# Layer 1's softmax divided on GpSimd before its product with the values, in a two-layer attention and feed-forward kernel

## The chip, the cores and the metric

The kernel runs on one core of a Trainium2 chip, in one launch. The metric is the device time of that launch in microseconds, the median of several runs. The engines are named as the profile names them: PE (TensorE, matmuls and transposes), PEld (its weight loads), DVE (VectorE), ACT (ScalarE), POOL (GpSimd) and SP (SyncE, which issues DMAs).

## The reference, cut to what matters

Input x has 2 batches of 2048 rows of 512 numbers, that is 32 tiles of 128 rows. Two layers follow each other. Each has attention over a context of 128 rows and then a feed-forward part; a layer norm stands ahead of each of the four. Layer 0 has attention with rotary embedding and a quantised feed-forward part. Layer 1 is where the change lies:

```python
Q, K, V = heads(q @ Wq.T + bq), heads(k @ Wk.T + bk), heads(v @ Wv.T + bv)   # 16 heads of 32
scores = einsum('bhqd,bhkd->bhqk', Q, K) / sqrt(32)
scores = where(mask, 1e-9, scores)
attn = softmax(scores, axis=-1)
ctx = einsum('bhqk,bhkd->bhqd', attn, V)
x = x + (ctx @ Wo.T + bo)
# then, on the norm of x:
probs = softmax(x @ Wg + bg)                  # 512 wide
idx = argmax(probs); p = probs[idx]; e = idx % 8
out = relu(x @ We[e] + be[e]) * p             # the expert of each row
x = x + out
```

All arithmetic around the change is in float32. A softmax is exponentials divided by their sum over the 128 keys; the division may be made before the product with V or after it.

## The kernel before, in words

The first part of the launch (layer 0, up to about 944 us) is not touched. From there to 1476 us the kernel runs 32 steps, n = 0 to 31, one for each tile of 128 rows. The rest is the experts' work.

The order of instructions on PE, DVE, ACT and POOL is that of the code in this part: the schedule is manual (L741), each engine takes its instructions in the order in which the step issues them, and waits on semaphores where it needs another engine's result. A step does the attention of tile n, the output projection and the norm of tile n-1, the gate of tile n-2, and the layer norm of a tile that comes four later. Its functions, in the order of the loop (L1160 on):

- `weighed(n-1)`: DVE multiplies the attention's output `po` of the last step by reciprocals (L897).
- `scores(n)`: 16 small matmuls into `sc` (L833); DVE masks them into the tiles `s1_0` and `s1_1`, 8 heads of 128 keys each (L841), and takes their maxima (L846).
- `queries`: PE's product for the next block of two tiles (L813); it comes twice in a step.
- `exponentials(n)`: ACT makes 16 exponentials of 128x128 (L855). Those of the first half add up their rows as they go, by an accumulator that is read after each; those of the second half do not.
- `projected(n-1)`: POOL adds the bias `bob` to the residual (L902), PE multiplies by the output weights (L905), DVE adds the product to the residual (L906).
- `normed2(n-1)`: DVE takes mean and variance, POOL raises the variance to the power -0.5 (L100), DVE centres the tile (L103).
- `kept_keys(n+1)`: DVE turns a mask's row into numbers (L823). `normed`: the same statistics, power and centring for a tile of the block after the next.
- `logits(n-2)`: PE's gate product (L928); DVE's maximum and index (L930 to L934).
- `summed(n)`: DVE sums the second half's rows (L859) and takes the reciprocal of all 16 sums (L861); POOL spreads them to 128x512 (L864).
- `gated(n-2)`: ACT's exponentials of the gate with their sum (L942); DVE's expert number, its one-hot row `hot` (L949) and the running count `cum` (L950).
- for n from 4 to 19, POOL adds a row to two 128x512 pieces of the experts' weights (L1204).
- `turned(n)`: PE transposes the exponentials, 16 of 128x128, in four groups (L115); ACT copies each group back into `s1_0` and `s1_1` (L874).
- `turned2(n-1)`: PE transposes the centred tile (L115), ACT copies it (L922).
- `mixed(n)`: PE transposes the spread reciprocals into `pr` (L883), multiplies the exponentials by the values into `po` (L887), and ACT copies `pr` to `oT` (L892).
- in odd steps up to 27, `turned1` transposes the two tiles of the block after the next.

In steps 24 to 27 pieces of the routing table follow at the step's end, on DVE for the most part; in steps 30 and 31 an expert's product takes the queries' place. PE's results go to PSUM, in a ring of four buffers of 128x512 that all these products share, besides `sc` with one buffer. POOL cannot take part in work on PSUM here: all its operands are tiles in SBUF.

Of the kernel before, what the change touches and what calls it, by code (L numbers as in the profile page):

```python
# [11 lines left out]
F32 = mybir.dt.float32  # L12
# [6 lines left out]
ALU = mybir.AluOpType  # L19
# [4 lines left out]
P = 128  # L24
# [38 lines left out]
def two_layers(ctx: ExitStack, tc: tile.TileContext, a, out):  # L63
# [86 lines left out]
    with ExitStack() as l0:  # L150
# [168 lines left out]
        def normed(k):  # L319


            for t, n in enumerate(tiles[k]):
                mv = variance(xs[n])
                ve = small.tile([P, 1], F32, name="ve")
                nc.vector.tensor_scalar(ve, mv[:, 1:2], 1.0 + EPS, EPS * EPS, ALU.mult, ALU.add)
                rr = small.tile([P, 1], F32, name="rr")
                nc.gpsimd.tensor_tensor(rr, ve, minus_half, ALU.pow)
                norms[k, t] = mv, rr
# [84 lines left out]
        def projected(u, t):  # L413

            k, g = divmod(u, NG)
            if g == 0:
                pws[k, t] = psq.tile([P, D], F32, name="pw", tag="pw", bufs=NB0)
            pw = pws[k, t]
            for f in range(2):
                nc.tensor.matmul(  # L420
                    pw, atts[u][:, f, t * P : (t + 1) * P], wo[:, 2 * g + f, :],
                    start=(g == 0 and f == 0), stop=(g == NG - 1 and f == 1),
                )
# [356 lines left out]
        nc.gpsimd.tensor_tensor(xs[n], xs[n], y, ALU.add)  # L780


    scs, xTs, qTs, keeps, ss_, sums, rw_, pTs_, mix, os_ = {}, {}, {}, {}, {}, {}, {}, {}, {}, {}
    xn1s = {}

    def normed(n):
# [62 lines left out]
    def exponentials(n):  # L849

        sums[n] = small.tile([P, 16], F32, name="sums")
        for half, (s, mx) in enumerate(ss_[n]):
            for h in range(8):
                accum = {} if half else {"accum_out": sums[n][:, h : h + 1]}
                nc.scalar.activation(s[:, h, :], s[:, h, :], AF.Exp, bias=mx[:, h : h + 1], **accum)  # L855

    def summed(n):

        nc.vector.tensor_reduce(sums[n][:, 8:], ss_[n][1][0], AX.X, ALU.add)  # L859
        rs = small.tile([P, 4, 4], F32, name="rs")  # L860
        nc.vector.reciprocal(rs, sums[n].rearrange("p (r c) -> p c r", c=4))  # L861

        rw_[n] = mid.tile([P, 4, P], F32, name="rw", bufs=1)
        nc.gpsimd.tensor_copy(  # L864
            rw_[n].rearrange("p c (r f) -> p c r f", f=DH1), rs.unsqueeze(3).to_broadcast([P, 4, 4, DH1])
        )

    def turned(n):

# [7 lines left out]
    def mixed(n):  # L877

        b, pTs = n // TPB, pTs_[n]
        pr = psm.tile([P, 4, P], F32, name="pr1", tag="m")  # L880
        po = psm.tile([P, 4, P], F32, name="po1", tag="m")
        for c in range(4):
            nc.tensor.transpose(pr[:, c, :], rw_[n][:, c, :], ident)  # L883
        for c in range(4):
            for r in range(4):
                h = 4 * c + r
                nc.tensor.matmul(  # L887
                    po[32 * r : 32 * r + 32, c, :], v1[b][:, h * DH1 : (h + 1) * DH1], pTs[r][:, c, :],
                    start=True, stop=True, tile_position=(0, 32 * r),
                )  # L890
        oT = mid.tile([P, 4, P], F32, name="oT", bufs=1)
        nc.scalar.copy(oT, pr)  # L892
        mix[n] = po, oT

    def weighed(n):
        po, oT = mix[n]
        nc.vector.tensor_tensor(oT, po, oT, ALU.mult)  # L897
        os_[n] = oT

    def projected(n):  # L900

        nc.gpsimd.tensor_tensor(xs[n], xs[n], bob, ALU.add)  # L902
        pw = psm.tile([P, D], F32, name="pw1", tag="m")
        for c in range(ND):
            nc.tensor.matmul(pw, os_[n][:, c, :], wo1[:, c, :], start=(c == 0), stop=(c == ND - 1))  # L905
        nc.vector.tensor_tensor(xs[n], xs[n], pw, ALU.add)  # L906
# [3 lines left out]
    def normed2(n):  # L910

        mv = variance(xs[n])
        nc.vector.tensor_copy(xw[n][:, D : D + 1], mv[:, 0:1])
        r = xw[n][:, D + 1 : D + 2]
        rsqrt_eps(r, mv[:, 1:2])
        xn2[n] = mid.tile([P, D], F32, name="xn2", bufs=1)
        return lambda: center(xn2[n], xs[n], mv[:, 0:1], r)
# [6 lines left out]
    def logits(n):  # L924

        pl = pls[n] = psm.tile([P, D], F32, name="pl", tag="m")
        for c in range(ND):
            nc.tensor.matmul(pl, xn2T[n][:, c, :], wgate[:, c, :], start=(c == 0), stop=(c == ND - 1))  # L928
        m8 = small.tile([P, 8], F32, name="m8")
        nc.vector.max(out=m8, in_=pl)  # L930
        negm = small.tile([P, 1], F32, name="negm")
        nc.vector.tensor_scalar(negm, m8[:, 0:1], -1.0, None, ALU.mult)
        i8 = small.tile([P, 8], U32, name="i8")
        nc.vector.max_index(out=i8, in_max=m8, in_values=pl)  # L934
        picks[n] = negm, i8

    def gated(n):

        negm, i8 = picks[n]
        pe = small.tile([P, 1], F32, name="pe1")  # L940

        nc.scalar.activation(  # L942
            scs[min(n + 2, NT - 1)][:, 0].rearrange("p c k -> p (c k)"), pls[n], AF.Exp, bias=negm, accum_out=pe
        )
        ei = small.tile([P, 1], U32, name="ei")
        nc.vector.tensor_scalar(ei, i8[:, 0:1], NE - 1, None, ALU.bitwise_and)
        ef = small.tile([P, 1], F32, name="ef")
        nc.vector.tensor_copy(ef, ei)
        nc.vector.tensor_scalar(hot[:, n, :], iota_e, ef, None, ALU.is_equal)  # L949
        nc.vector.tensor_tensor(cum[:, n + 1, :], cum[:, n, :], hot[:, n, :], ALU.add)  # L950
        nc.vector.memset(xw[n][:, D + 3 : D + 4], 0.0)

        def rest():
            nc.vector.reciprocal(xw[n][:, D + 2 : D + 3], pe)
            nc.sync.dma_start(out=x_dram[n * P : (n + 1) * P, :], in_=xw[n])

        return rest
# [202 lines left out]
    for n in range(NT):  # L1160
        blk, t = n // NB1, n % NB1
        ahead = blk + 1 < nblk
        fs = range(t * ND // NB1, (t + 1) * ND // NB1)
        if n > 0:
            weighed(n - 1)
        scores(n)
        if ahead:
            queries(blk + 1, fs[:1])
        exponentials(n)
        if n == 0:  # L1170
            for i in range(NT - held, NT - held + 2):
                down(i)
                widened(i + 2)
        if n > 0:
            projected(n - 1)
            rest2 = normed2(n - 1)
        if n + 1 < NT:
            kept_keys(n + 1)
        rest1 = normed((blk + 2) * NB1 + t) if blk + 2 < nblk else None
        if n > 0:  # L1180
            rest2()
        if n > 1:
            logits(n - 2)
        summed(n)
        rest = gated(n - 2) if n > 1 else None
        if rest1:
            rest1()
        if ahead:
            queries(blk + 1, fs[1:])
        if n == 0:  # L1190
            for i in range(NT - held + 2, NT):
                down(i)
            dwn.close()
            ffd.close()
            moe = ctx.enter_context(tc.tile_pool(name="moe", bufs=1, side="right"))
            we = moe.tile([P, NE, ND, D], F32, name="we")
            for e in range(NE):
                load(we[:, e], a["L1_ffn_We"][e].rearrange("(c p) f -> p c f", p=P))
        if 4 <= n < 4 + 2 * NE:
            e, half = divmod(n - 4, 2)  # L1200
            if half == 0:
                load(rowadd, v_dram[e].partition_broadcast(P))
            for c in range(2 * half, 2 * half + 2):
                nc.gpsimd.tensor_tensor(we[:, e, c, :], we[:, e, c, :], rowadd, ALU.add)  # L1204
        if not ahead:

            expert(n - NT + NB1)
        turned(n)
        if rest:
            rest()  # L1210
        if n > 0:
            turned2(n - 1)
        mixed(n)
        if t == NB1 - 1 and blk + 2 < nblk:
            for t in range(NB1):
                turned1((blk + 2) * NB1 + t)
        if n == NTA + 2:
            route = routing(True)
        if route:
            for _ in range(3 if n == NTA + 2 else 2):  # L1220
                if next(route, route) is route:
                    route = None
                    for j in range(4):
                        gathered(j)
                    break
        if n == NT - NB1 - 1:
            for j in range(2):
                centered_x(j)
            turned_x2(0)
    weighed(NT - 1)  # L1230
    projected(NT - 1)
    normed2(NT - 1)()
    logits(NT - 2)
# [50 lines left out]
```

## Time and profile before

| what | time |
| --- | --- |
| median of 3 runs | 1643.19 us (1642.39 to 1645.04) |
| the profiled execution | 1642.48 us |
| its span, first to last instruction | 1640.8 us |
| 32 attention steps of layer 1 | 944 to 1476 us |
| step 20, scores to scores | 15.74 us |
| step 21 (odd: two more tiles turned) | 16.77 us |
| mean granted clock of TensorE | 0.998 |

The profile is one execution. A row gives an engine's instruction with its source line, what it writes and reads, and its duration. Matmuls are pipelined, so a PE row's duration overlaps the next one; the distance between starts tells what a piece of work takes of PE. "Waits" say which engine's semaphore ended an idle time.

### The profile page before, as it was taken

How to read it: one execution, taken by the hardware profiler on the slowest of the kernel's cores; microseconds unless marked ns; L12 is line 12 of the kernel's file. 1: busy time of each engine (PE TensorE's matmuls, PEld its weight loads, DVE VectorE, ACT ScalarE, POOL GpSimd, SP SyncE). 2: the span in 40 equal slices, each digit the busy share in tenths (PEclk: the TensorE clock that was granted, in tenths of full speed). 3: DMA queues.
4: the chain of work that ended last, by engine and by line, in shares of the span. 5: the costliest groups of instructions: out<-in, count | busy, mean ns of one | idle time of the engine just before them, and what ended most of it. 6: DMA issues, size and time to landing. Idle time of an engine off the chain costs nothing. (4 is left out here: it accounts for less than half of the span.)

```text
span 1640.8 us, 26515 instructions
## 1 busy us (share of the span) xinstructions
PE 1597.7 (97%) x9962; PEld 952.5 (58%) x9962; DVE 1185.9 (72%) x2290; ACT 686.3 (42%) x1539; POOL 437.5 (27%) x498
## 2 busy tenths in 40 slices
PE   7999999999999999989999999999999999999997
PEld 5666666665666666534443566666666666654543
DVE  3466666777777765689986678898999889876332
ACT  1222222222222222234436576666666665662332
POOL 2322222222222221110005632333333221224553
PEclk9999999999999999999999999999999999999999
DMA  9400111010100220556658650001000000113332
GB/s 318 151 17 22 28 26 27 20 27 20 27 20 14 54 37 1 161 161 183 186 175 294 235 204 16 27 20 33 21 27 20 21 14 21 40 47 103 125 124 67
DMA packets 123883, 128.61 MB, mean 78 GB/s; under 512 B 43857, under 2 KB 91433, under 8 KB 123756
## 3 DMA queue, kind: packets, MB, share of 16 engines
q1 hardware_dynamic: 114508, 107.03, 21.2%
q0 software_dynamic: 6240, 18.70, 3.6%
q8 instruction: 80, 1.31, 0.3%
q10 hardware_dynamic: 3008, 1.19, 0.3%
q14 instruction: 47, 0.39, 0.1%
HBM read 78.96 MB, written 41.76 MB: 74 GB/s over the span
## 5 line engine op out<-in xcount | busy, mean ns | idle before, releaser
L362 PE MATMUL pq<-xnT,wq 128*128 128x256 f32 x1024 | 254.4, 392 | 0.0
L420 PE MATMUL pw<-wo,att 128*128 128x512 f32 x512 | 230.9, 593 | 0.0
L362 PEld LDWEIGHTS pq<-xnT,wq 128*128 128x128 f32 x1024 | 184.6, 190 | 66.9 <-issue 46.7
L855 ACT ACTIVATE s<-s,mx 128x128 f32<-128x128 f32 x512 | 176.7, 387 | 18.1 <-DVE mx L846 18.1
L388 ACT ACTIVATE pr<-sc 128x1024 f32<-128x1024 f32 x64 | 65.5, 1024 | 237.8 <-PE sc L383 234.7
L372 POOL TENSOR_TENSOR q<-rt,rt 128x256 f32<-128x256 f32 x64 | 46.5, 726 | 410.5 <-DVE rt L371 410.5
L420 PEld LDWEIGHTS pw<-wo,att 128*128 128x128 f32 x512 | 97.0, 190 | 96.2 <-issue 89.8
L410 DVE RECIPROCAL rd<-sc 128x256 f32<-128x256 f32 x64 | 112.5, 1757 | 51.1 <-PE sc L404 51.1
L1119 PE MATMUL pz<-we,x 128*128 x312 | 140.7, 594 | 0.6 <-issue 0.5
L813 PE MATMUL pq<-xT,wq 128*128 128x256 f32 x512 | 124.1, 385 | 0.0
L347 ACT ACTIVATE xnT<-pt,lnb,lng 128x256 f32<-128x256 f32 x64 | 32.6, 559 | 216.1 <-PE pt L345 216.1
L367 DVE TENSOR_TENSOR rt<-pq,rope_cos 128x256 f32<-128x256 f32 x64 | 27.2, 425 | 130.8 <-PE pq L362 120.2
L905 PE MATMUL pw<-wo,oT 128*128 128x512 f32 x256 | 115.5, 594 | 1.6 <-DVE oT L897 1.6
L928 PE MATMUL pl<-wgate,xnT 128*128 128x512 f32 x256 | 115.1, 592 | 0.0
L813 PEld LDWEIGHTS pq<-xT,wq 128*128 128x128 f32 x512 | 94.9, 190 | 28.0 <-issue 13.6
L716 ACT ACTIVATE gate<-pg,gsc 128x512 f32<-128x512 f32 x88 | 60.5, 687 | 96.5 <-PE pg L711 85.8
L711 PE MATMUL pu<-xqT,wuT 128*128 128x512 bf16 x352 | 90.3, 379 | 5.3 <-DVE h L719 5.3
L91 DVE BATCH_NORM_STATS2 st<-x 128x6 f32<-128x512 f32 x130 | 89.6, 689 | 5.6 <-DMA x<-in_ctx 3.4
L841 DVE SCALAR_TENSOR_TENSOR s<-sc,keep 128x1024 f32<-128x1024 f32 x64 | 77.9, 1217 | 20.6 <-PE sc L833 20.6
L1123 DVE TENSOR_TENSOR x<-x,x 128x512 f32<-128x512 f32 x39 | 27.0, 692 | 90.0 <-ACT x L1122 89.8
L711 PE MATMUL pg<-xqT,wgT 128*128 128x512 bf16 x352 | 90.3, 379 | 0.0
L1119 PEld LDWEIGHTS pz<-we,x 128*128 128x128 f32 x312 | 56.4, 190 | 58.2 <-issue 57.9
(218 smaller groups left out, 2847.7 us busy)
## 6 DMA issues: line engine op xcount, KB each, us to landing
h_dram<-h SPq DMA_DIRECT2D x88, 256.0 KB
hq<-h_dram SPq DMA_DIRECT2D x31, 704.0 KB
x_dram<-x SPq DMA_DIRECT2D x32, 258.0 KB
x<-in_x SPq DMA_DIRECT2D x32, 256.0 KB
we<-in_L_ffn_We SPq DMA_DIRECT2D x8, 1024.0 KB
w_in<-in_L_ffn_w_gate SPq DMA_DIRECT2D x11, 256.0 KB
w_down<-in_L_ffn_w_down SPq DMA_DIRECT2D x4, 704.0 KB
w_in<-in_L_ffn_w_up SPq DMA_DIRECT2D x11, 256.0 KB
```

The lines of the kernel that those rows point to most:

```text
L91: nc.vector.bn_stats(out=st, in_=x)
L362: nc.tensor.matmul(pq, wqs[c // 2][:, c % 2, par, g * P : (g + 1) * P], xnTs[k][:, c, :], start=(c == 0), stop=(c == ND - 1))
L388: nc.scalar.activation(pr, sc[:, :, :B0], AF.Tanh, scale=1.0 / (math.sqrt(DH0) * GROK))
L410: nc.vector.reciprocal(rd, sc[:, 0, B0:])
L420: nc.tensor.matmul(pw, atts[u][:, f, t * P : (t + 1) * P], wo[:, 2 * g + f, :], start=(g == 0 and f == 0), stop=(g == NG - 1 and f == 1),)
L711: nc.tensor.matmul(dst, w[:, c, i * P : (i + 1) * P], xqTs[blk][:, c, :], start=(c == 0), stop=(c == ND - 1),)
L813: nc.tensor.matmul(pq, wq1[:, c, f * P : (f + 1) * P], xTs[blk][:, c, :], start=(c == 0), stop=(c == ND - 1))
L841: nc.vector.scalar_tensor_tensor(s, sc[:, 2 * half : 2 * half + 2].rearrange("p r c k -> p (r c) k"), -MASKED, keeps[n].unsqueeze(1).to_br ...
L855: nc.scalar.activation(s[:, h, :], s[:, h, :], AF.Exp, bias=mx[:, h : h + 1], **accum)
L905: nc.tensor.matmul(pw, os_[n][:, c, :], wo1[:, c, :], start=(c == 0), stop=(c == ND - 1))
L928: nc.tensor.matmul(pl, xn2T[n][:, c, :], wgate[:, c, :], start=(c == 0), stop=(c == ND - 1))
L1119: nc.tensor.matmul(pz, ring[j][:, c, :], we[:, bass.ds(e, 1), c, :], start=(c == 0), stop=(c == ND - 1))
```

## The change

The exponentials themselves are divided by their sums before they are transposed, on POOL, one product for each half of the heads; the reciprocals are no longer spread, turned and copied. ACT's accumulators now go with the second half, and DVE sums the first. The output projection's PSUM result is copied by ACT alone, and `weighed` is gone. In a step the gate's product now comes ahead of the output's, the bias is added in a function of its own ahead of the two products on POOL, and the centring of tile n-1 follows its statistics at once. `kept_keys` and the other norm's statistics come after the gate. The counts of experts (`cum`) are added by POOL.

```diff
-    def summed(n):
-        nc.vector.tensor_reduce(sums[n][:, 8:], ss_[n][1][0], AX.X, ALU.add)
-        rs = small.tile([P, 4, 4], F32, name="rs")
-        nc.vector.reciprocal(rs, sums[n].rearrange("p (r c) -> p c r", c=4))
-        rw_[n] = mid.tile([P, 4, P], F32, name="rw", bufs=1)
-        nc.gpsimd.tensor_copy(
-            rw_[n].rearrange("p c (r f) -> p c r f", f=DH1), rs.unsqueeze(3).to_broadcast([P, 4, 4, DH1])
-        )
+    def shares(n, half):
+        s, sm = ss_[n][half][0], sums[n][:, 8 * half : 8 * half + 8]
+        if half == 0:
+            nc.vector.tensor_reduce(sm, s, AX.X, ALU.add)
+        rs = small.tile([P, 8], F32, name="rs")
+        nc.vector.reciprocal(rs, sm)
+        nc.gpsimd.tensor_tensor(s, s, rs.unsqueeze(2).to_broadcast([P, 8, T]), ALU.mult)
...
     def mixed(n):
-        pr = psm.tile([P, 4, P], F32, name="pr1", tag="m")
         po = psm.tile([P, 4, P], F32, name="po1", tag="m")
-        for c in range(4):
-            nc.tensor.transpose(pr[:, c, :], rw_[n][:, c, :], ident)
...
-        oT = mid.tile([P, 4, P], F32, name="oT", bufs=1)
-        nc.scalar.copy(oT, pr)
-        mix[n] = po, oT
-
-    def weighed(n):
-        po, oT = mix[n]
-        nc.vector.tensor_tensor(oT, po, oT, ALU.mult)
-        os_[n] = oT
+        os_[n] = mid.tile([P, 4, P], F32, name="oT", bufs=1)
+        nc.scalar.copy(os_[n], po)
+
+    def biased(n):
+        nc.gpsimd.tensor_tensor(xs[n], xs[n], bob, ALU.add)
...
-        nc.vector.tensor_tensor(cum[:, n + 1, :], cum[:, n, :], hot[:, n, :], ALU.add)
+        nc.gpsimd.tensor_tensor(cum[:, n + 1, :], cum[:, n, :], hot[:, n, :], ALU.add)
...
-        if n > 0:
-            weighed(n - 1)
         scores(n)
         if ahead:
             queries(blk + 1, fs[:1])
         exponentials(n)
...
         if n > 0:
+            biased(n - 1)
+        shares(n, 0)
+        if n > 1:
+            logits(n - 2)
+        if n > 0:
             projected(n - 1)
-            rest2 = normed2(n - 1)
+        shares(n, 1)
+        if n > 0:
+            normed2(n - 1)()
+        rest = gated(n - 2) if n > 1 else None
+        rest1 = normed((blk + 2) * NB1 + t) if blk + 2 < nblk else None
         if n + 1 < NT:
             kept_keys(n + 1)
-        rest1 = normed((blk + 2) * NB1 + t) if blk + 2 < nblk else None
-        if n > 0:
-            rest2()
-        if n > 1:
-            logits(n - 2)
-        summed(n)
-        rest = gated(n - 2) if n > 1 else None
         if rest1:
             rest1()
```

After the last step `biased` takes the place of `weighed`.

More of the change, by code (lines that the diff above doesn't have):

```diff
@@ L780, in down @@
         nc.gpsimd.tensor_tensor(xs[n], xs[n], y, ALU.add)
-    scs, xTs, qTs, keeps, ss_, sums, rw_, pTs_, mix, os_ = {}, {}, {}, {}, {}, {}, {}, {}, {}, {}
+    scs, xTs, qTs, keeps, ss_, sums, pTs_, os_ = {}, {}, {}, {}, {}, {}, {}, {}
     xn1s = {}
@@ L853, in exponentials @@
             for h in range(8):
-                accum = {} if half else {"accum_out": sums[n][:, h : h + 1]}
+                accum = {"accum_out": sums[n][:, 8 + h : 9 + h]} if half else {}
                 nc.scalar.activation(s[:, h, :], s[:, h, :], AF.Exp, bias=mx[:, h : h + 1], **accum)
-    def summed(n):
-        nc.vector.tensor_reduce(sums[n][:, 8:], ss_[n][1][0], AX.X, ALU.add)
-        rs = small.tile([P, 4, 4], F32, name="rs")
-        nc.vector.reciprocal(rs, sums[n].rearrange("p (r c) -> p c r", c=4))
-        rw_[n] = mid.tile([P, 4, P], F32, name="rw", bufs=1)
-        nc.gpsimd.tensor_copy(
-            rw_[n].rearrange("p c (r f) -> p c r f", f=DH1), rs.unsqueeze(3).to_broadcast([P, 4, 4, DH1])
-        )
+    def shares(n, half):
[5 more added lines that the diff above has]
+        nc.gpsimd.tensor_tensor(s, s, rs.unsqueeze(2).to_broadcast([P, 8, T]), ALU.mult)
     def turned(n):
@@ L890, in mixed @@
                 )
-        oT = mid.tile([P, 4, P], F32, name="oT", bufs=1)
-        nc.scalar.copy(oT, pr)
-        mix[n] = po, oT
-    def weighed(n):
-        po, oT = mix[n]
-        nc.vector.tensor_tensor(oT, po, oT, ALU.mult)
-        os_[n] = oT
+        os_[n] = mid.tile([P, 4, P], F32, name="oT", bufs=1)
+        nc.scalar.copy(os_[n], po)
+    def biased(n):
+        nc.gpsimd.tensor_tensor(xs[n], xs[n], bob, ALU.add)
     def projected(n):
-        nc.gpsimd.tensor_tensor(xs[n], xs[n], bob, ALU.add)
         pw = psm.tile([P, D], F32, name="pw1", tag="m")
@@ L1229, in two_layers @@
             turned_x2(0)
-    weighed(NT - 1)
+    biased(NT - 1)
     projected(NT - 1)
```

## The prediction

> **What bounds the kernel now.** I read the page's busy shares first, then the busy time by stretches, then the order of time of one step on each engine, and last who waited for whom between 944 and 1476 us, the 32 steps of layer 1's attention that the diff touches. In that stage the rows have TensorE (PE) idle almost never. The page (busy us, share of the span, instructions) and two stretches (length, then busy us of each engine):
>
> ```profile
> PE 1597.7 (97%) x9962; PEld 952.5 (58%) x9962; DVE 1185.9 (72%) x2290; ACT 686.3 (42%) x1539; POOL 437.5 (27%) x498
> ```
> ```profile
> 1025.53:1289.22 263.69, 261.49 (x1989) 175.82 (x1988) 237.86 (x450) 171.61 (x561) 92.41 (x96) 1.00 0.08 24
> 1273.50:1338.50 65.00, 65.00 (x501) 44.02 (x500) 56.19 (x112) 42.58 (x140) 13.09 (x17) 1.00 0.06 20
> ```
>
> PE fills all 65.00 us of four steps; VectorE (DVE) 56.19, GpSimd (POOL) 13.09. So a step is as long as PE's list of work, as long as nothing that PE needs comes late. Step 20 on PE, in order of time (start, us, engine, line):
>
> ```profile
> 1273.45 1.17 PE L833 MATMUL sc<-kT,qT 32*128 32x128 f32 x32
> 1274.55 1.99 PE L813 MATMUL pq<-xT,wq 128*128 128x256 f32 x8
> 1276.38 3.60 PE L905 MATMUL pw<-wo,oT 128*128 128x512 f32 x8
> 1279.82 3.60 PE L928 MATMUL pl<-wgate,xnT 128*128 128x512 f32 x8
> 1283.25 1.89 PE L813 MATMUL pq<-xT,wq 128*128 128x256 f32 x8
> 1284.98 2.02 PE L115 MATMUL pt<-ident,s 128*128 128x128 f32 x16
> 1286.83 0.60 PE L115 MATMUL pt<-ident,xn 128*128 128x128 f32 x4
> 1287.32 0.63 PE L883 MATMUL pr<-ident,rw 128*128 128x128 f32 x4
> 1287.87 1.39 PE L887 MATMUL po<-s,v 128*32 128x128 f32 x32
> 1289.19 1.17 PE L833 MATMUL sc<-kT,qT 32*128 32x128 f32 x32
> ```
>
> From scores to scores is 15.74 us without a gap. An odd step adds two turned tiles of the next block and takes 16.77 (step 21), or 17.22 in the odd steps from 5 to 19, where the experts' additions (L1204) run on POOL. There DVE's centring L103 takes 1.57 instead of 0.54, and PE waits 0.26 for it. POOL's rows, then DVE's:
>
> ```profile
> 1269.96 2.50 POOL L1204 TENSOR_TENSOR we<-we,rowadd 128x512 f32<-128x512 f32 x2
> ...
> 1287.16 1.28 POOL L902 TENSOR_TENSOR x<-x,bob 128x512 f32<-128x512 f32 x1
> ```
> ```profile
> 1271.18 1.57 DVE L103 TENSOR_SCALAR xn<-x,mv,r 128x512 f32<-128x512 f32 x1
> ...
> 1287.27 1.20 DVE L950 TENSOR_TENSOR cum<-cum,hot 128x8 bf16<-128x8 bf16 x1
> 1288.40 0.54 DVE L103 TENSOR_SCALAR xn<-x,mv,r 128x512 f32<-128x512 f32 x1
> ```
>
> The reader is to see that the count L950 ends when POOL's L902 ends (1288.47 against 1288.44; with POOL idle it takes 0.16), and the centring when the second L1204 is done. These DVE forms stand still while POOL adds.
>
> **The change, part by part, in step 20.** Times are from the start of its scores; the odd and the special steps follow. All in us.
>
> *Removed from PE:* four transposes of the spread reciprocals (L883), 1287.32 to 1287.87, 0.55 a step, at most 32 x 0.55 = 17.6. DVE loses the product L897 (0.68) and the count (0.16 to 1.2), POOL the spreading copy (0.61). DVE and POOL are off the path, and what PE lost to L897 was 2.8 in all 32 steps, so these count as nothing. ACT's copy of pr becomes one of po: same count.
>
> *Exchanged:* gate's product is now second (at 2.93), the output's third (at 6.37, ending at 9.97). Same rows, no PE time. DVE's list follows it: sum of the first half, its reciprocal, gate's maximum and index, the output's addition, the second reciprocal.
>
> *Added, and on the path:* two POOL products of 128x1024. No row has this. Nearest: 128x256 takes 0.73 (L372) and 128x512 1.27 (L1204), so 0.54 per 256 more: 1.27 + 2 x 0.54 = **2.35**, my value. Bounds: 1.20, twice L864's copy of 512 (0.60), which reads a broadcast, as this does beside its first input; 3.4, if it is stretched as L780 was beside DVE's casts (1.85 against 1.27); an added product can't take less than nothing, so no gain lies below.
>
> The chain, by rows: exponentials begin at 3.81; the half without sums takes 2.43 and ends at 6.24, the other, with accumulator reads, 3.10 and 9.34. DVE sums the first half (1.20) at 6.30 to 7.50, takes its reciprocal to 7.70 (0.20, between 0.15 for one element and 0.25 for 16), POOL starts 0.17 later (as L864 after L861): first product 7.87 to 10.22. PE wants it at 11.53: hidden, with 1.3 to spare. The second reciprocal stands behind the addition, which waits for the output's product: 9.97 + 0.10, addition 0.60, reciprocal 0.20, POOL at 11.04, product to 13.39. PE wants it after the first eight transposes, at 11.53 + 0.93 = 12.46, and gets it at 13.49: a **wait of 1.03** that did not exist. Behind PE's waiting transpose stands all PE work.
>
> On POOL, the power for the norm of tile n-1 (L100, 0.55) stands behind this product: 13.94, centring to 14.51. PE's turned norm, ready at 14.42, waits to 14.60, ends 15.09. The values' product then meets ACT's last copy (transposes in at 14.1, copies 0.6 and 0.5: 15.25), some 0.2 more: 15.09 + 1.15 (L887 without waits, step 30) + 0.2 = 16.45. So an even step is 16.45 - 15.74 = **+0.7**.
>
> In an odd step PE also needs the second new tile centred. DVE now does this last: after 14.5 come the three picks (0.57), statistics (1.1), power on POOL (0.55), centring: 17.4. The count on POOL, between L100's 0.55 and L902's 1.28, is issued at 15.0 and hides behind those statistics, which end at 16.2; at 1.28 it would cost 0.1. PE would be there at 16.97: turned 17.45 to 17.97, say 17.9 against 16.77, **+1.1**. In steps 5 to 19 POOL goes straight from that power to L1204 (its rows follow each other without a gap), while DVE begins 0.03 after the power (rows at 1415): I take the centring as held for one addition, 1.25, so 19.0 against 17.22, **+1.8**; if DVE gets in first, +0.7.
>
> The Trainium skill has the rule for this, page "SBUF — State Buffer", section "Who interferes with whom": VectorE's two-port modes and its operations with two SBUF inputs exclude GpSimd's, and whichever starts first keeps the shared port to its end. L950 and L103 above agree; no row shows who wins when both wait for the same power. By the rule with POOL first the sum is the one below, with DVE first it is 8 x 1.1 = 9 less.
>
> *Moved:* the mask's row, statistics and reciprocals to the step's end on DVE; queues of SP keep their order. The hidden parts cost if DVE's end slips past the next scores (17.2 against 17.75): then the first product's 1.3 of slack takes it.
>
> The sum: steps 4 to 19, 8 pairs x (0.7 + 1.8) = 20.0; steps 2, 3, 20 to 23, 3 pairs x 1.8 = 5.4; routing steps 24 to 27, 2 x 1.8 = 3.6; 28 and 29, 2 x 0.7 = 1.4; PE's stalls on ACT's gate exponentials (1.7 + 3.1 in the rows) mostly go, with gate first, -2. Step 1 has no gate product, so the second product follows the first, to 12.65 with transposes ready at 9: 16.65 against 15.05, +1.6. Step 0 has `down` as cover, +0.2. In 30 and 31 an expert's 3.4 covers the second product, -0.3 each. Total **+29.6**. The profiled execution took 1642.48 (span 1640.8), 0.7 under the median 1643.19 of the runs shown: 1642.48 + 29.6 = **1672**.
>
> **Rivals.**
> 1. *Faster: POOL multiplies at its copy's pace*, 1.20 instead of 2.35. For it: in1 is a broadcast, as in L864. Against: L372 and L1204, both with two inputs. The second product then ends at 12.24, before 12.46, and nothing waits for it; an even step gains 0.5, an odd one nothing (the centring is still last), or loses 0.7 with L1204. 8 x (+0.2) - 5 x 0.5 - 1.0 - 2 + 1.0 - 0.6 is about -3.5: **1639**. It decides below some 1.4 a product.
> 2. *Milder: DVE gets in ahead of L1204 and the product takes 2.05.* Each step 0.3 less, -9, and the race -9: **1653**.
> 3. *Heavier: the product is stretched to 3.3 or more*, as L780 was. For it: L780's rows; against: the DVE forms beside the product (maximum, index, addition from PSUM, statistics) show 0.69 with POOL busy and idle. +0.95 x 32 = 30 more: **1702**.
> 4. *Nothing to tell:* 1640 to 1646, between 1 and 2, a product of about 1.6.
>
> **How the numbers follow.** Forecast (1658 to 1686) 0.65; rival 1, 0.08; rival 2 (1646.5 to 1658) 0.12; rival 3 (1686 to 1710) 0.11; rival 4, 0.04. The range 1648 to 1698 leaves out rivals 1 and 4 and the ends of 2 and 3, some 0.2. Within 0.2%, 3.3 us, is about what a measurement of this kernel can't tell from no change: faster 0.08, same 0.04, slower 0.88.
>
> **What would show it.** POOL's products (on L864 of the changed kernel too) as 64 rows near 2.35; PE's transposes of the second half waiting about 1.0 in nearly every step, released by POOL; turned norm waiting on DVE, 0.2; odd steps 5 to 19 near 19.0 with L103 at some 1.6 right after L100; step 20 near 16.45. Wrong if L864 is under 1.5, or if PE's transposes wait for no one.

## The result, and the profile after

The changed kernel took **1666.53 us** (median of four runs, 1664.97 to 1667.26) against 1643.36 for the kernel before beside it: a ratio of **1.0146**, 95% interval 1.0133 to 1.0158 (the two medians alone give 1.0141). The forecast was 1672, its range 1648 to 1698. The profiled execution took 1664.97, its span 1663.2. From the scores of step 0 to those of step 31 it needs 535.0 us instead of 511.0; the stage therefore holds all of the loss (span +22.4; the part ahead of the stage is 1.9 shorter in this execution, the part behind it 0.4 longer).

The page of the changed kernel: busy us, share of the span and instructions, and further down the group of the new products.

```profile
PE 1588.8 (96%) x9810; PEld 940.1 (57%) x9834; DVE 1140.5 (69%) x2258; ACT 700.7 (42%) x1539; POOL 539.4 (32%) x562
...
L864 POOL TENSOR_TENSOR s<-s,rs 128x1024 f32<-128x1024 f32 x64 | 121.3, 1897 | 225.8 <-DVE rs L863 218.2
```

PE has 8.9 us less to do, DVE 45.4 less, and the span is longer; POOL has 101.9 more, 121.3 of it the products, 1.90 us each and not 2.35. So no engine ran out: PE waits. The same stretch that was read ahead of the prediction (length, then busy us of each engine):

```profile
1025.53:1289.22 263.69, 244.79 (x1886) 162.71 (x1886) 199.36 (x417) 171.68 (x532) 139.46 (x127) 1.00 0.08 24
```

PE's 261.49 busy us have become 244.79 at the same clock: 7% of the stretch is idle. Who ended the waits in 944 to 1500 us (us in total, times, longest):

```profile
POOL s L864 <- DVE rs L863: 218.2, 60, 10.1
DVE xn L103 <- POOL x L100: 47.4, 31, 1.6
...
PE pt L115 <- POOL s L864: 18.0, 32, 1.7
...
PE pt L115 <- DVE x L945: 16.1, 13, 1.3
```

PE has two waits that matter, both of transposes. The one for the divided exponentials (POOL) is new; the one for VectorE, now in 13 odd steps, was 2.1 in 8 before. The last row names a reciprocal, L945; the tile that PE transposes comes from the centring just ahead of it on DVE, as the rows show. PE from the end of step 19 through step 20, in order of time:

```profile
1284.52 0.66 PE L115 MATMUL pt<-ident,xn 128*128 128x128 f32 x4
1286.51 0.63 PE L115 MATMUL pt<-ident,xn 128*128 128x128 f32 x4 [1.33 <-DVE x L945]
1287.06 1.17 PE L833 MATMUL sc<-kT,qT 32*128 32x128 f32 x32
...
1298.59 1.04 PE L115 MATMUL pt<-ident,s 128*128 128x128 f32 x8
1300.06 1.09 PE L115 MATMUL pt<-ident,s 128*128 128x128 f32 x8 [0.43 <-POOL s L864]
1301.24 0.63 PE L115 MATMUL pt<-ident,xn 128*128 128x128 f32 x4
1301.79 1.20 PE L882 MATMUL po<-s,v 128*32 128x128 f32 x32
1302.92 1.17 PE L833 MATMUL sc<-kT,qT 32*128 32x128 f32 x32
```

POOL, then DVE, in the same time:

```profile
1284.29 0.55 POOL L100 TENSOR_TENSOR r<-ve,minus_half 128x1 f32<-128x1 f32 x1 [0.74 <-DVE ve L99]
1284.81 2.68 POOL L1195 TENSOR_TENSOR we<-we,rowadd 128x512 f32<-128x512 f32 x2
1287.45 1.27 POOL L890 TENSOR_TENSOR x<-x,bob 128x512 f32<-128x512 f32 x1
1295.04 1.90 POOL L864 TENSOR_TENSOR s<-s,rs 128x1024 f32<-128x1024 f32 x1 [6.32 <-DVE rs L863]
1298.11 1.90 POOL L864 TENSOR_TENSOR s<-s,rs 128x1024 f32<-128x1024 f32 x1 [1.17 <-DVE rs L863]
1299.96 0.55 POOL L100 TENSOR_TENSOR x<-ve,minus_half 128x1 f32<-128x1 f32 x1
1301.75 0.20 POOL L941 TENSOR_TENSOR cum<-cum,hot 128x8 bf16<-128x8 bf16 x1 [1.25 <-DVE hot L940]
1302.70 0.55 POOL L100 TENSOR_TENSOR r<-ve,minus_half 128x1 f32<-128x1 f32 x1 [0.74 <-DVE ve L99]
1303.21 1.27 POOL L890 TENSOR_TENSOR x<-x,bob 128x512 f32<-128x512 f32 x1
```
```profile
1284.88 1.48 DVE L103 TENSOR_SCALAR xn<-x,mv,r 128x512 f32<-128x512 f32 x1 [0.53 <-POOL r L100]
...
1297.13 0.69 DVE L897 TENSOR_TENSOR x<-x,pw 128x512 f32<-128x512 f32 x1 [0.84 <-PE pw L896]
1297.74 0.20 DVE L863 RECIPROCAL rs<-sums 128x8 f32<-128x8 f32 x1
...
1303.28 1.48 DVE L103 TENSOR_SCALAR xn<-x,mv,r 128x512 f32<-128x512 f32 x1 [0.53 <-POOL r L100]
```

Step 20 starts at 1287.06. The second product starts 11.05 later, behind the output's addition L897 and the reciprocal L863 as forecast (11.04), and ends at 12.95. PE waits 0.43 for it, and 0.25 more goes between the second half's transposes and the turned norm (1300.06 to 1301.24 is 1.18; eight transposes take 0.93), since the norm's power L100 stands behind the product. With the 0.55 saved an even step is 15.86: 0.12 more than before. At the step's end the power for the new tile comes, and with it two instructions at once: POOL's next addition (1303.21) and DVE's centring (1303.28). The centring takes 1.48 instead of 0.55. It does so beside the bias L890 too, in a step without the experts' additions. All odd steps from 3 to 23 are 18.4.

### The profile page after: what moved, and what is told of

It is laid out like the page before. It is cut to its first block, busy times and chain, and to the rows that moved or that the text cites. A ratio compares the mean times of both kernels' runs of the same rounds, so it can differ in the third digit from the quotient of the medians.

```text
span 1663.2 us, 26364 instructions
## 1 busy us (share of the span) xinstructions
PE 1588.8 (96%) x9810; PEld 940.1 (57%) x9834; DVE 1140.5 (69%) x2258; ACT 700.7 (42%) x1539; POOL 539.4 (32%) x562
## 3 DMA queue, kind: packets, MB, share of 16 engines
q10 hardware_dynamic: 3008, 1.19, 0.3%
## 5 line engine op out<-in xcount | busy, mean ns | idle before, releaser
L864 POOL TENSOR_TENSOR s<-s,rs 128x1024 f32<-128x1024 f32 x64 | 121.3, 1897 | 225.8 <-DVE rs L863 218.2
L388 ACT ACTIVATE pr<-sc 128x1024 f32<-128x1024 f32 x64 | 65.6, 1024 | 237.7 <-PE sc L383 234.7
```

Of the source, the lines that this page charges most:

```text
L864: nc.gpsimd.tensor_tensor(s, s, rs.unsqueeze(2).to_broadcast([P, 8, T]), ALU.mult)
```

## The experiments

**Theory.** The loss is made by two places in the order, not by the products' length: the second reciprocal stands behind the output's addition, and the new tile's centring is last on DVE and is held by POOL's next addition. **Rivals:** the products fill POOL or get in DVE's way wherever they stand; the bias has no part in the odd steps; the swap of the gate's and the output's product is what costs. Lengths of steps below are scores to scores in each kernel's profile; ratios are to the kernel before, run on the same chip.

**1. The bias after the centring.** The bias of a tile is added right behind its centring, not ahead of the products (the first tiles keep theirs).

```diff
-        if n > 0:
+        if 0 < n <= 2 * NB1:
             biased(n - 1)
...
             rest1()
+            biased((blk + 2) * NB1 + t)
...
-    biased(NT - 1)
```

> The bias of a tile is added once the tile is centred (it waits for the centring), so GpSimd has nothing to start right behind the norm's power; all else as in the changed kernel, whose even steps take 15.86 us and odd ones 18.40. Theory (the odd steps are late because GpSimd's next addition gets in ahead of VectorE's centring and holds it for 1.27 us): the centring falls from 1.48 to 0.55 us where no expert's addition follows, and also where one does, since the bias now stands between; odd steps 17.45, 13 to 14 of them, about 13 us off, 1653 us. Rival (the odd steps are late because the power itself comes late, the holding only fills time that PE would wait anyway): odd steps stay within 0.2 of 18.40, 1664 to 1667 us.

Measured: 1653.77, ratio 1.006 (1.0042 to 1.0078). Even steps 15.79, odd ones 17.40 throughout, those with the experts' additions too, which now come behind the bias. The rows of DVE and of POOL:

```profile
1246.51 0.55 DVE L103 TENSOR_SCALAR xn<-x,mv,r 128x512 f32<-128x512 f32 x1 [0.53 <-POOL r L100]
```
```profile
1245.92 0.55 POOL L100 TENSOR_TENSOR r<-ve,minus_half 128x1 f32<-128x1 f32 x1 [0.75 <-DVE ve L99]
1247.13 1.27 POOL L890 TENSOR_TENSOR x<-x,bob 128x512 f32<-128x512 f32 x1 [0.66 <-DVE x L945]
```

With nothing on POOL right behind the power the centring is 0.55 again, and an odd step 1.0 shorter. So the addition that follows the power holds the centring, and the bias does it as well as the experts' addition. The Trainium skill, page "SBUF — State Buffer", section "Who interferes with whom", lets whichever of the two engines starts first have the port that they share, until it ends. The rows agree: POOL was first by 0.07 wherever both waited for one power.

**2. The second division ahead of the output's addition.**

```diff
+        shares(n, 1)
         if n > 0:
             projected(n - 1)
-        shares(n, 1)
```

> The second half's reciprocal and product are issued ahead of the output projection, so that the reciprocal no longer stands behind the addition that waits for PE. Theory (the place of the reciprocal in VectorE's order makes PE's wait, not the length of the product): the second product follows the first at 9.9 us of a step and ends at 11.8, ahead of PE's 12.46; PE's transposes wait for no product; even steps 15.2; odd steps still wait about 1.2 for the held centring, 17.45; about 22 to 24 us off, 1643 us. Rival (the products as such hold the step up, wherever they stand): even steps stay above 15.7, 1660 us or more.

Measured: 1649.46, ratio 1.0036 (1.0026 to 1.0046). Even steps 15.32, odd 17.54; PE waits for a product 7 times instead of 32. The mechanism is as the theory has it; the time is 6 above the expectation. In part the steady steps are each 0.1 above it (15.2 and 17.45), in part the first two steps (19.50 and 16.69) and steps 25 and 27 (20.06 and 19.69) stayed long.

**3. The new tile's norm ahead of the gate's picks.**

```diff
-            normed2(n - 1)()
-        rest = gated(n - 2) if n > 1 else None
+            rest2 = normed2(n - 1)
         rest1 = normed((blk + 2) * NB1 + t) if blk + 2 < nblk else None
-        if n + 1 < NT:
-            kept_keys(n + 1)
+        if n > 0:
+            rest2()
         if rest1:
             rest1()
+        rest = gated(n - 2) if n > 1 else None
+        if n + 1 < NT:
+            kept_keys(n + 1)
```

> The statistics and the power of the new tile's norm are put back ahead of the gate's picks, into the time in which VectorE waits for the other power, and both centrings follow each other; the second product stays where it is. Theory (odd steps are late because the new tile's norm was moved to the end of the step): the centring of the new tile is done by 14.6 us of the step, PE's second turned tile waits for nothing, odd steps 16.9 to 17.0; even steps stay 15.86, with the wait of 0.43 for the second product; about 20 us off, 1646 us. Rival (the added products set both steps): odd steps stay near 18.4, 1664 us or more.

Measured: 1645.25, ratio 1.0013 (1.0003 to 1.0023). Odd steps 16.88, even ones still 15.86; steps 25 and 27 fall from 20.64 and 19.94 to 17.68 and 17.13. DVE's two centrings now follow one another:

```profile
1254.35 0.55 DVE L103 TENSOR_SCALAR xn<-x,mv 128x512 f32<-128x512 f32 x1 [0.52 <-POOL x L100]
1254.96 0.55 DVE L103 TENSOR_SCALAR xn<-x,mv,r 128x512 f32<-128x512 f32 x1
```
```profile
1254.28 0.65 POOL L100 TENSOR_TENSOR r<-ve,minus_half 128x1 f32<-128x1 f32 x1
1256.17 0.20 POOL L941 TENSOR_TENSOR cum<-cum,hot 128x8 bf16<-128x8 bf16 x1 [1.25 <-DVE keep L823]
1256.33 2.50 POOL L1197 TENSOR_TENSOR we<-we,rowadd 128x512 f32<-128x512 f32 x2
```

The count `cum`, which waits for the gate's picks, now stands on POOL between the power and the additions, and keeps them off the centring. This one place in DVE's list is worth 1.5 us in each odd step.

**4. The products left out.** Sums and reciprocals stay, the exponentials are not divided.

```diff
-        nc.gpsimd.tensor_tensor(s, s, rs.unsqueeze(2).to_broadcast([P, 8, T]), ALU.mult)
```

> The two products on GpSimd are left out (the exponentials are not divided by their sums); sums and reciprocals stay. Theory (their whole cost is the one wait of PE and the later power, which the second kernel of this call removes by order alone): even steps 15.2, odd 17.4, 1643 us, within 3 us of the kernel with the second product ahead. Rival (the products also slow VectorE and the rest through the port that they share): this kernel is 8 us or more below that one, 1635 us or less.

Measured: 1643.17, ratio 0.9999 (0.999 to 1.0009). This is 6.3 under experiment 2, between the two expectations, and alone it would decide nothing. The steps do: even ones are 15.26 against 15.32, odd ones 17.54 in both. The stage is 5.3 shorter than in experiment 2 (511.5 against 516.8): step 0 has 1.6 of it, step 1 0.85, steps 25 to 27 0.6 each, and each even step 0.06. In the steady steps the products cost next to nothing once the second reciprocal is early, so the first rival falls there; in the first two steps they do cost.

**5. Both moves** (the diffs of 2 and 3 together).

> Both orders together: the second product ahead of the output projection, and the new tile's norm ahead of the gate's picks. Theory (the two waits are separate: 0.54 us of every step and 1.5 us of every odd step, and with both gone the step is PE's list without the four transposes): even steps 15.3 and odd ones 16.3, 1628 to 1633 us, below the kernel before (0.991 to 0.994 of it). Rival (with PE's waits gone another engine, VectorE with its list or GpSimd's additions at the step's end, sets the step): even steps above 15.6 or odd ones above 16.7, 1638 us or more.

Measured: **1631.96, ratio 0.9935 (0.9922 to 0.9949)**, faster than both kernels. Even steps 15.32, odd 16.34, against 15.74 and 16.77 to 17.22 before. PE through an odd step, without a wait:

```profile
1251.76 1.17 PE L833 MATMUL sc<-kT,qT 32*128 32x128 f32 x32
...
1263.29 1.91 PE L115 MATMUL pt<-ident,s 128*128 128x128 f32 x16
1265.32 0.63 PE L115 MATMUL pt<-ident,xn 128*128 128x128 f32 x4
1265.88 1.27 PE L882 MATMUL po<-s,v 128*32 128x128 f32 x32
1267.08 1.09 PE L115 MATMUL pt<-ident,xn 128*128 128x128 f32 x8
1268.11 1.17 PE L833 MATMUL sc<-kT,qT 32*128 32x128 f32 x32
```

All 16 transposes stand in one row. An even step has lost its 0.55 for the turned reciprocals but for 0.13. So the change pays once these two places are put right, 0.65% of the time; the two places cost 2.1% (0.9935 to 1.0146), three times as much. Not all of the 0.65% comes from the division: the counts on POOL, which are part of the change, give the kernel before 0.25% by themselves (experiment 7).

**6. The swap undone.** The output's product is ahead of the gate's again, all else as in the changed kernel.

```diff
-        if n > 1:
-            logits(n - 2)
         if n > 0:
             projected(n - 1)
         shares(n, 1)
         if n > 0:
             normed2(n - 1)()
+        if n > 1:
+            logits(n - 2)
```

> One part undone: the output's product comes ahead of the gate's again, as before the change; all else as in the changed kernel (gate's maximum and index now follow the norm of the tile before). Theory (the exchange made the second reciprocal late, since the addition ahead of it waits for the output's product): PE waits for no second product, even steps 15.3 to 15.4, odd ones still late by the centring, 17.5 or, since gate's picks now come later on VectorE, up to 18.0; 1649 to 1656 us. Rival (the exchange costs nothing; the product's length does): even steps stay 15.8 or more, 1664 us or more.

Measured: 1744.72, ratio 1.0623 (1.0606 to 1.0639), steps of 18.5 to 20.5: far above either expectation. Its greatest wait of PE from 944 to 1520 us, and PE's rows in one step:

```profile
PE pt L115 <- ACT sc L933: 71.7, 26, 4.2
```
```profile
1345.89 1.04 PE L115 MATMUL pt<-ident,s 128*128 128x128 f32 x8
1349.62 1.06 PE L115 MATMUL pt<-ident,s 128*128 128x128 f32 x8 [2.69 <-ACT sc L933]
```

L933 is ACT's exponential of the gate, which reads the gate's product in PSUM and waits for DVE's maximum and index. With the gate's picks behind the norm these come late, the product keeps one of the four PSUM buffers, and the transposes of the second half wait for it, not for POOL (2 waits instead of 32). In this order the early gate is therefore a gain: it frees a buffer. That was in neither expectation.

The kernel before has the same order of the two products, with the picks behind the norm, and does not wait like this: in step 19 the maximum starts 0.07 after the gate's product ends (1266.28). Here it starts 2.8 after (1347.10), since the centring ahead of it on DVE waits for a power that stands on POOL behind the second division. So the loss belongs to this order together with the divisions. The edit moves the picks as well as the product; the swap of the two products alone was not tested.

**7. The counts on GpSimd, and nothing else,** in the kernel before.

```diff
-        nc.vector.tensor_tensor(cum[:, n + 1, :], cum[:, n, :], hot[:, n, :], ALU.add)
+        nc.gpsimd.tensor_tensor(cum[:, n + 1, :], cum[:, n, :], hot[:, n, :], ALU.add)
```

> Of the change only the counts on GpSimd, in the kernel before. Theory (whichever engine starts first keeps the other out): the centring of the new tile now follows the one-hot row at once and starts ahead of the experts' additions, so it takes 0.5 to 0.6 us instead of 1.57; odd steps 5 to 19 fall from 17.22 to 16.76, 8 times 0.46 is 3.7 us off, 1639.5 us (0.9978). Rival (VectorE is off the path, and the count of 0.2 us on GpSimd changes nothing): 1642 to 1645 us, odd steps stay 17.2.

Measured: 1638.48, ratio 0.9975 (0.9966 to 0.9984). Odd steps 5 to 19 fall from 17.22 to 16.77. DVE's centring, then POOL's rows:

```profile
1250.25 0.54 DVE L103 TENSOR_SCALAR xn<-x,mv,r 128x512 f32<-128x512 f32 x1
```
```profile
1250.47 0.37 POOL L950 TENSOR_TENSOR cum<-cum,hot 128x8 bf16<-128x8 bf16 x1 [0.17 <-DVE x L951]
1250.80 2.50 POOL L1204 TENSOR_TENSOR we<-we,rowadd 128x512 f32<-128x512 f32 x2
```

The centring takes 0.54: the count waits for DVE, stands ahead of L1204 in POOL's list, and so keeps the experts' additions off it. It does what it did in experiment 3. DVE also loses the count itself, which took 1.20 ahead of the centring beside the first addition; the two gains were not separated. In the changed kernel the same count comes ahead of the power and keeps nothing off.

**8. A second input of full size.** Each half is multiplied by itself; nothing is divided, and the products no longer need the reciprocals.

```diff
-        nc.gpsimd.tensor_tensor(s, s, rs.unsqueeze(2).to_broadcast([P, 8, T]), ALU.mult)
+        nc.gpsimd.tensor_tensor(s, s, s, ALU.mult)
```

> The products' second input is the tile itself instead of a broadcast of one number per 128 (the exponentials are squared and not divided). Theory (a second input that changes only every 128 elements is read faster, which is why the product took 1.90 us and not the 2.35 drawn from rows with two full inputs): the product takes 2.3 to 2.4 us, PE's wait for the second one grows from 0.43 to about 0.9, even steps 16.3. Rival (two inputs cost 1.90 at this length whatever they are; the line through 256 and 512 elements was drawn too steep): the product stays 1.85 to 1.95 us and the steps as in the changed kernel.

Measured: 1.89 a product (1887 to 1897 ns), 1646.02 in one run. By this the broadcast is not what makes the product shorter than forecast, a reading that experiment 10 narrows. Beside it: even steps are 15.32 and odd ones 17.54, as in experiment 2, with products of the same length. What they wait for makes the wait.

**9. Two lengths.** Half 0 takes two products of 512 by the broadcast, half 1 an addition of 1024 in place of its product, so its exponentials are not divided.

```diff
-        nc.gpsimd.tensor_tensor(s, s, rs.unsqueeze(2).to_broadcast([P, 8, T]), ALU.mult)
+        if half == 0:
+            for q in range(2):
+                v = s[:, 4 * q : 4 * q + 4, :]
+                nc.gpsimd.tensor_tensor(v, v, rs[:, 4 * q : 4 * q + 4].unsqueeze(2).to_broadcast([P, 4, T]), ALU.mult)
+        else:
+            nc.gpsimd.tensor_tensor(s, s, rs.unsqueeze(2).to_broadcast([P, 8, T]), ALU.add)
```

> The first half is divided by two products of 512 elements instead of one of 1024, and the second half's product is an addition of 1024 with the same broadcast (so the second half is not divided). It measures the term that was mis-sized. Theory (a product costs less per element than an addition on GpSimd): products of 512 take about 0.95 us, the addition of 1024 about 2.35 to 2.5. Rival (time bends with the length, whatever the operation: 1.27 for 512 and 1.90 for 1024): products of 512 take 1.2 to 1.3, the addition of 1024 1.85 to 1.95. Third (the additions in the kernel before, with two full inputs in other tiles, are slower by their operands' places): 0.95 and 1.90.

POOL's groups of this kernel (busy us and mean ns of one, then idle time ahead of them):

```profile
L867 POOL TENSOR_TENSOR s<-s,rs 128x512 f32<-128x512 f32 x64 | 65.3, 1041 | 201.7 <-DVE rs L863 194.1 <-ACT s L855 7.2 <-ACT qT L816 0.5
L869 POOL TENSOR_TENSOR s<-s,rs 128x1024 f32<-128x1024 f32 x32 | 60.7, 1897 | 20.6 <-DVE rs L863 19.9 <-POOL s L867 0.4
```

One run, 1668.66. An addition is as long as a product, so the operation is not it; from 512 to 1024 the length grows by 0.86, which leaves 0.18 that does not grow. None of the three expectations has both lengths; the third is nearest. That still did not fit the additions of 512, which take 1.27.

**10. Two full inputs.** The first half is multiplied by the second, the second by the bias tile in two rows of 512; nothing is divided.

```diff
-        nc.gpsimd.tensor_tensor(s, s, rs.unsqueeze(2).to_broadcast([P, 8, T]), ALU.mult)
+        if half == 0:
+            nc.gpsimd.tensor_tensor(s, s, ss_[n][1][0], ALU.mult)
+        else:
+            for q in range(2):
+                v = s[:, 4 * q : 4 * q + 4, :].rearrange("p h t -> p (h t)")
+                nc.gpsimd.tensor_tensor(v, v, bob, ALU.mult)
```

> What sets the length of a two-input operation on POOL? So far: a product of 1024 by a broadcast 1.90, of a tile by itself 1.89, an addition of 1024 with a broadcast 1.90, a product of 512 by a broadcast 1.04; but additions of 512 with another full tile 1.27 and products of 256 of two full tiles 0.73. Left out here: the division (the products have other second inputs, so the output is not the reference's). The first half is multiplied by the second half, one row of 1024 with two different full tiles, the second half by the bias tile in two rows of 512. Theory (a second input that is another full tile costs more than a broadcast or the same tile): the 1024 takes 2.3 to 2.4, the two of 512 1.27 each; then the forecast's 2.35 was right for the rows that it was taken from, and wrong for a broadcast. Rival (the additions of 512 are slow for their place, right behind a power or beside VectorE, not for their input): 1.90 and 1.04. Time of the whole: by either 1665 to 1690, since the second half's rows stand at the same place and take 2.1 to 2.5.

```profile
L869 POOL TENSOR_TENSOR s<-s,bob 128x512 f32<-128x512 f32 x64 | 80.1, 1271 | 2.5
L865 POOL TENSOR_TENSOR s<-s,s 128x1024 f32<-128x1024 f32 x32 | 75.2, 2350 | 250.7 <-ACT s L855 250.7
```

This settles the length: 2.35 and 1.27 with another full tile as second input, 1.90 and 1.04 with a broadcast. The forecast's working (1.27 + 2 x 0.54) was right to the hundredth for the rows that it was taken from; those rows had two full inputs, and the change has not. The time of the whole, 1723.43 in one run, misses the expectation: the first product now reads the second half as well and starts only when ACT is done with that, which was overlooked.

## Why the prediction was right, and which steps of it failed

The sign, the place and the two mechanisms were right, and the time is within the forecast's own bounds (1658 to 1686). That the sum came so near is partly luck: its errors had both signs (added us, scores to scores):

| steps | forecast | measured |
| --- | --- | --- |
| 4 to 19 | 20.0 | 10.4 |
| 2, 3, 20 to 23 | 5.4 | 5.3 |
| 24 to 27 | 3.6 | 4.8 |
| 28, 29 | 1.4 | 0.2 |
| 0, 1 | 1.8 | 3.3 |
| 30, 31 | -0.6 | 0.0 (30 alone) |
| gate stalls, not given to a step | -2.0 | in the rows above |
| sum | 29.6 | 24.0 |

- *"The second reciprocal stands behind the addition"*: right to 0.01 in its start, and experiment 2 removes the wait with it. *"Wait of 1.03"* was 0.43: mis-sized by the term *"two POOL products of 128x1024"*, 2.35 where 1.90 came (experiments 8 to 10). It is the main reason for +0.12 instead of +0.7 in even steps. The turned norm's wait of 0.2 came (0.25). The 0.2 for the values' product did not.
- *"PE's stalls on ACT's gate exponentials (1.7 + 3.1 in the rows)"*: the stalls did go, but the 3.1 are the weight loads' waits (PEld) in the same stalls, so that PE had 1.7 to gain; the 2.8 for L897 is added up in the same way from 1.6 and 1.2.
- *"0.55 a step"* for the removed transposes: 0.48 without products (experiment 4), and 0.42 with them in good places (experiment 5).
- *Odd step, "+1.1"*: failed, 1.65 in steps 3, 21 and 23. That DVE centres last was right (experiment 3 takes it away). But the text sent POOL from the power to an addition only where L1204 is; the bias, moved by the same diff to the next place on POOL, holds the centring just as well (experiment 1). Two errors met here: without the hold the step is 17.40 (experiment 1) where the forecast had 17.9, and the hold adds 1.0.
- *"I take the centring as held for one addition"*: right, POOL is first in every step; 1.48 against 0.55. The +1.8 for steps 5 to 19 is 1.19. Most of the difference is that the chain is earlier: in step 21 the centring of tile n-1 ends 14.03 after the scores, not 14.51, close to what the shorter product gives (0.45); the hold is 0.93 and not 1.25.
- *Steps 24 to 27*: 25 and 27 lost 2.1 and 2.8, not 1.1. The text named the case, *"if DVE's end slips past the next scores"*, and took it not to come. It came in steps 25 and 27. There DVE goes from the centring into the routing's pieces and masks the scores 4.5 and 3.8 after they start (3.6 and 2.3 in the kernel before), and PE waits for both products. In step 25, DVE, then PE:

```profile
1371.81 1.48 DVE L103 TENSOR_SCALAR xn<-x,mv,r 128x512 f32<-128x512 f32 x1 [0.53 <-POOL r L100]
...
1376.18 1.22 DVE L841 SCALAR_TENSOR_TENSOR s<-sc,keep 128x1024 f32<-128x1024 f32 x1
```
```profile
1384.81 1.09 PE L115 MATMUL pt<-ident,s 128*128 128x128 f32 x8 [1.41 <-POOL s L864]
1386.93 1.97 PE L115 MATMUL pt<-ident,s 128*128 128x128 f32 x8 [1.03 <-POOL s L864]
```

  With the centring early (experiment 3) DVE is done sooner, and both steps fall to about the length of before (17.68 and 17.13 against 18.51 and 17.15).
- *"Step 0 has `down` as cover, +0.2"*: failed, +1.6. Without products it is 17.89 as before. `down` does not cover them, because the power of a norm stands behind both on POOL (it starts at 957.15), DVE's centring waits 2.31 for it, and behind the centring stands DVE's read of a product of `down` (L779); PE's transposes of the second half wait 1.42 for that read. Step 1 was forecast at +1.6 and is +1.74; 0.95 of it goes with the products.
- *"The count on POOL"*, said to hide behind the statistics: 0.20, hidden. That it gains 3.9 us in the kernel before (experiment 7), by keeping additions off a centring, was not seen.
- Of the rivals, 1 wanted under 1.4 a product; 2 had 2.05 and DVE ahead, and got the nearer length and the wrong winner; 3 failed, no product was stretched.

## What to carry to other kernels

When work goes from a full engine to an idle one, its length hardly matters while it is covered; look at what its start stands behind in each engine's list, and at what now comes last. Two instructions on VectorE and GpSimd that wait for the same result can be a race, which GpSimd won here each time by 0.07: put on the engine that is to come second an instruction that waits for something later, ahead of its long one. And take a duration from a row with the same kind of second input, not only the same size.

## What the runs showed of the hardware

- GpSimd, two inputs in float32, 128 partitions: another full tile 0.73, 1.27 and 2.35 for 256, 512 and 1024 elements; a broadcast 1.04 and 1.90 for 512 and 1024; a tile by itself 1.89 for 1024. That the second stream's reads are the cause is argued only.
- TensorE's granted clock fell after short waits. In experiment 6, ahead of, in and behind the stretch that follows an idle time of 2.69 us (length, busy us of the engines, granted clock behind them):

```profile
1345.90:1349.60 3.70, 1.02 (x9) 0.80 (x8) 2.82 (x10) 0.90 (x3) 0.86 (x3) 1.00 0.00 0
1349.60:1353.70 4.10, 4.08 (x48) 3.15 (x48) 2.33 (x6) 2.77 (x6) 1.83 (x3) 0.62 0.07 27
1353.70:1357.00 3.30, 3.30 (x42) 2.91 (x42) 1.85 (x2) 0.64 (x2) 0.00 (x0) 0.95 0.13 47
```

  The clock's own records have 22 such periods in that stage, each 3.41 us long at half speed, where PE has 30 waits of 2.68 or more. The changed kernel has two, in steps 1 and 25 (with waits of 1.67 and 0.77, and of 1.41 and 1.03); the kernel before has none in the stage. In step 25 the second transposes above take 1.97 for that reason and not 1.09. Experiment 2 has no such period, and its steps 1 and 25 are still 1.64 and 1.55 above those of before, so the clock is not what made these two steps long. The Trainium skill, page "TensorE: Matmul & The Clock Gate", section "Part 1: The HAM clock gate", asks for an idle window of about 3.4 us; here 2.69 was enough. So a part of the 78 us by which experiment 6 is above the changed kernel may be clock and not wait; how much was not measured. Half of 22 periods of 3.41 is 38, an upper estimate.
